# The tail of a two-layer graph network: the sums of the next tile ordered ahead of W's product, additions on VectorE, and a second set of row buffers

## Chip, cores and metric

One Trainium2 chip, one core, one program. The metric is the device time of one execution in microseconds: the median of three runs is 2738.88 us (2735.98 to 2744.72).

## The reference, cut to what matters

x has 32 batches of 512 nodes with 512 features; adj is one random 512 x 512 matrix with about four neighbours per node. There are two layers, each behind a layernorm and a relu, each added to x:

```python
# layer 0: masked attention, 8 heads of 64
h = maximum(layernorm(x), 0)
x = x + softmax(q k^T / 8 + (1 - adj) * -1e9) v  @ Wo
# layer 1: graph attention with a multiplied mask
h = maximum(layernorm(x), 0)
hw = h @ W;  s1 = hw @ a1;  s2 = hw @ a2
e = leaky_relu(s1[:, None] + s2[None, :], 0.2) * adj
x = x + elu(softmax(e) @ hw + beta * hw)
```

In layer 1 the mask multiplies e, so nodes that are not neighbours weigh exp(0) = 1. The kernel writes the weighted sum as the sum of all states of the batch plus, for each neighbour, (exp(e) - 1) times its state, and puts the product with W after the sum.

## The kernel before, in words

**Tiles.** A batch has four tiles of 128 nodes. For each tile the kernel gathers, from tables in device memory, the rows of its nodes' neighbours (GpSimd's indirect DMAs, L946, four a tile, into two "kv" buffers), and in layer 0 also the queries (L968, four a tile, into two "qe" buffers). A row of the table holds K, V and, from column HO on, the layer-1 part: one score and the 512 values of the state h, padded to HW_ = 520 columns (ROW = 1552).

**Periods.** `stage_b` runs through periods b = 0 to 33. Period b works on layer 0 of batch b and layer 1 of batch b - 2 (LAG = 2), tile by tile; tile n is 4b + t. The last two periods, tiles 128 to 135, have layer 1 alone, of batches 30 and 31, and gather the state rows only, from the table th.

**Layer 1 of a tile** (`edge_weights`, `layer1`):
- VectorE adds s1 to the gathered score (L1127, once per kv buffer), leaky relu (L1131); ScalarE exp (L1133); VectorE completes z (L1134), copies it into the rows where layer 0 needs it (L1138) and spreads it to the weights wv (L1140).
- TensorE multiplies wv with the gathered states, four matmuls with 32 columns of weights each (L987, "sums"), and in the last two periods wv with ones (L42 128x1, "count").
- VectorE makes the denominator (L1162 to L1164, "den") and adds the tile's own state (L1170, "own"). ScalarE had put its relu into the same buffer (L756).
- TensorE turns the result (L737, four transposes). ScalarE adds the column sums of the batch, cs, in four instructions of 128x128 (L1181, `add_all`) and so brings it to SBUF as gT.
- TensorE multiplies gT with W (L42, 128x512, eight matmuls). ScalarE scales in two passes (L1190, L1191, `halves`), VectorE does elu and adds x (L1195, L1196), GpSimd issues the store (L767, `keep`).

**Layer 0 of a tile**: product with the queries (L1000), reduction (L1003), exp (L1009), V weighed on ScalarE (L1014), sums "px" (L987), division (L1042, L1038), transposes, oT copied by ScalarE (L1051), product with wo (L42), addition (L1053), layernorm (L744 to L751, with its pow on GpSimd, L749), relu (L756), scores (L1061) and the store into the table. When all four tiles of a batch are through, `self_sums` adds up its states on TensorE (L1081) and cs is reduced (L1087); `spread_s1` sends the scores s1 through memory (SP, L1103 and L1108) to the form in which z needs them (L1112, L1113).

**What sets the order.** Every operation is given to a planner (`Plan`, L65 to L215) with its engine, an estimated time, a key (its due time), and the buffers it reads and writes. A tile has S = 20 of key: tile n begins at kb = base(n) = 100 + 20n. `order` runs a greedy list schedule over the estimated times and takes on each engine the ready operation with the lowest key; what comes out is the fixed order of each engine. Buffers come from rings: five "kv", two "qe", four "w", six PSUM banks "D", one "gT", one "oT", two "wv". On PSUM's ring any free one is taken, on the other rings allocations follow the keys. TensorE's list has a preference for staying with matmuls of the same form (32 or 128 rows).

Before the change the keys of layer 1 are: gathers kb - 17, z kb + 12 (0.6 S), sums, count, den, own kb + 20 (S), transposes and addition kb + 29.7 (+ 0.485 S), product kb + 37.6 (+ 0.88 S), halves and elu kb + 41 (+ 1.05 S), store kb + 44.

Of the kernel before, what the change touches and what calls it, by code (L numbers as in the profile page):

```python
# [12 lines left out]
ALU = mybir.AluOpType  # L13
# [6 lines left out]
P = 128  # L20
# [7 lines left out]
G = 32  # L28
# [1 line left out]
MAXDEG = 16  # L30
VW = 65
KO, VO, HO = 0, 512, 512 + 8 * VW
HW_ = 520
ROW = HO + HW_
QW = 516
LAG = 2
# [182 lines left out]
def kernel(  # L219
# [486 lines left out]


    S = 20.0
    AHEAD = 6

    def base(n):
# [222 lines left out]
    def stage_b(b):  # L934

        s = st[b] if b < B else None
        old = st[b - LAG] if b >= LAG else None
        if old is not None:
            old["dn"] = buf("dn", f"dn{b}")
        if s is not None:  # L940
            s["x1"], s["hx"] = [None] * T, [None] * T
            s["mv1"], s["s1"] = buf("mv1", f"mv1_{b}"), buf("s1", f"s1_{b}")
            s["rd"] = buf("rd", f"rd{b}")

        def gather(dst, tab, t, g):
            nc.gpsimd.indirect_dma_start(  # L946
                dst, None, tab.ap, bass.IndirectOffsetOnAxis(ap=idx[:, t, g : g + 1], axis=0),
                bounds_check=N + DUMMY - 1, oob_is_err=False,
            )

        for t in range(T):
            kb = base(T * b + t)
            slots = [buf("kv", f"kv{b}_{t}_{i}") for i in range(2)]
            held = [{n: buf(None, n) for n in ("K", "V", "H")} for _ in range(2)]
            of = {KO: "KVH", VO: "VH", HO: "H"}
            for g in range(NG):
                for tab, c0, c1 in st[b]["tab"]:
                    op("POOL", 1.3, kb - 0.85 * S + 0.1 * g, lambda sl=slots[g // 2], g=g, t=t, tab=tab, c0=c0, c1=c1: gather(
                        sl.ap[:, g % 2, c0:c1], tab, t, g),
                       r=[tab, C_["idx"]],  # L960
                       w=[(slots[g // 2], (g % 2, c0)), *((held[g // 2][n], (g % 2, "row")) for n in of[c0])],
                       dma=P * (c1 - c0) * 4)
            if s is not None:
                qs = [buf("qe", f"qe{b}_{t}_{i}") for i in range(2)]
                for q in qs:
                    q.q, q.s1 = buf(None, "q"), buf(None, "s1")
                for g in range(NG):
                    op("POOL", 1.3, kb - 0.84 * S + 0.1 * g, lambda q=qs[g // 2], g=g, t=t: nc.gpsimd.indirect_dma_start(  # L968
                        q.ap[:, g % 2, :], None, s["qtab"].ap,
                        bass.IndirectOffsetOnAxis(ap=qidx[:, t, g : g + 1], axis=0),  # L970
                        bounds_check=N, oob_is_err=False),
                       r=[s["qtab"], C_["qidx"]], w=[(x, g % 2) for x in (qs[g // 2], qs[g // 2].q, qs[g // 2].s1)],
                       dma=P * QW * 4)
            wvb = edge_weights(b - LAG, t, kb, slots, held, qs if s is not None else None) if old is not None else None
            pv = layer0(b, t, kb, slots, held, qs, old is not None) if s is not None else None
            if old is not None:
                layer1(b - LAG, t, kb, slots, held, wvb, pv)
                if t == T - 1:
                    op("DVE", 0.16, kb + 1.6 * S, lambda: nc.vector.tensor_tensor(
                        dmax, dmax, old["dn"].ap[:, 0:2, :], op=ALU.max), r=[old["dn"]], w=[C_["dmax"]])  # L980
        if s is not None:
            self_sums(b, base(T * b + 6))
# [136 lines left out]
    def edge_weights(b, t, kb, slots, held, qs):  # L1119

        s = st[b]
        k1 = kb + 0.6 * S
        z, wvb = buf("z", f"z{b}_{t}"), buf("wv", f"wv{b}_{t}")
        for i in range(2):
            def add(i=i):
                s1 = s["s1e"].ap[:, t, 2 * i : 2 * i + 2] if qs is None else qs[i].ap[:, :, D]
                nc.vector.tensor_tensor(z.ap[:, 2 * i : 2 * i + 2], s1, slots[i].ap[:, :, HO], op=ALU.add)  # L1127

            op("DVE", 0.2, k1, add, r=[*([s["s1e"]] if qs is None else [(qs[i], "use"), qs[i].s1]),
                                       *use([slots[i]], [held[i]], "H")], w=[z])  # L1130
        op("DVE", 0.2, k1, lambda: nc.vector.scalar_tensor_tensor(  # L1131
            z.ap, z.ap, ALPHA, z.ap, op0=ALU.mult, op1=ALU.max), w=[z])
        op("ACT", 0.25, k1, lambda: nc.scalar.activation(z.ap, z.ap, AF.Exp), w=[z])  # L1133
        op("DVE", 0.2, k1, lambda: nc.vector.scalar_tensor_tensor(  # L1134
            z.ap, z.ap, -1.0, nzE[:, t, :], op0=ALU.add, op1=ALU.mult), r=[C_["nzE"]], w=[z])
        if b + LAG < B:
            for i in range(2):
                op("DVE", 0.1, k1, lambda i=i: nc.vector.tensor_copy(  # L1138
                    slots[i].ap[:, :, HO], z.ap[:, 2 * i : 2 * i + 2]), r=[z, (slots[i], "use")], w=[(held[i]["H"], "z")])
        op("DVE", 0.35, k1, lambda: nc.vector.tensor_tensor(  # L1140
            wvb.ap.rearrange("p (g r) -> p g r", r=G), oh[:, ts(t, NG), :],
            z.ap.unsqueeze(2).to_broadcast([P, NG, G]), op=ALU.mult), r=[z, C_["OH"]], w=[wvb])
        return wvb

    def layer1(b, t, kb, slots, held, wvb, pv):
        s = st[b]
        px, g = buf("D", f"pg{b}_{t}"), buf("w", f"g{b}_{t}")
        o = op("PE", 1.02, kb + S, lambda: edge_sums(
            lambda i: px.ap[ts(i, G), :], lambda i: wvb.ap[:, ts(i, G)], slots, HO + 1, D),
               r=[*((x, "use") for x in slots), *((h["H"], "rows") for h in held), wvb], w=[px], form=4)  # L1150
        plan.reserve(o, g)
        k = kb + S
        x1, dn = s["x1"][t], s["dn"]
        op("ACT", 0.8, k, lambda: relu(g.ap, x1.ap, s["mv1"].ap, t), r=[x1, (s["mv1"], t)], w=[g])

        if pv is None:
            pd = buf("D", f"pn{b}_{t}")
            op("PE", 0.2, kb + S, lambda: product(nc, pd.ap[:, 0:1], wvb.ap, one32[:, 0:1]), r=[wvb], w=[pd])

        def den():  # L1160
            src, by = (pd.ap[:, 0:1], float(G)) if pv is None else (pv.ap[:, 1, 4 * VW : 4 * VW + 1], 1.0)
            nc.vector.tensor_scalar(dn.ap[:, 0, t : t + 1], src, by, float(N), op0=ALU.mult, op1=ALU.add)  # L1162
            nc.vector.reciprocal(dn.ap[:, 1, t : t + 1], dn.ap[:, 0, t : t + 1])
            nc.vector.tensor_scalar(  # L1164
                dn.ap[:, 2, t : t + 1], dn.ap[:, 0, t : t + 1], beta_b, 1.0, op0=ALU.mult, op1=ALU.mult)

        op("DVE", 0.5, k, den, r=[pd if pv is None else pv], w=[(dn, t)])

        def own():
            nc.vector.scalar_tensor_tensor(  # L1170
                g.ap, g.ap, dn.ap[:, 2, t : t + 1], px.ap, op0=ALU.mult, op1=ALU.add
            )

        op("DVE", 0.75, k, own, r=[px, (dn, t)], w=[g])
        pt, gT, py, y = buf("D", "pt"), buf("gT", f"gT{b}_{t}"), buf("D", "py"), buf("w", f"y{b}_{t}")
        oo = op("PE", 0.45, k + 0.485 * S, lambda: turned(pt.ap, g.ap), r=[g], w=[pt])
        plan.reserve(oo, gT)

        def add_all():
            for c in range(C):  # L1180
                nc.scalar.activation(  # L1181
                    gT.ap[:, c, :], pt.ap[:, ts(c, P)], AF.Identity, bias=s["cs"].ap[:, c : c + 1]
                )

        op("ACT", 1.5, k + 0.485 * S, add_all, r=[pt, s["cs"]], w=[gT])
        oo = op("PE", 3.43, k + 0.88 * S, lambda: dense(py.ap, gT.ap, w1), r=[gT, C_["w1"]], w=[py])
        plan.reserve(oo, y)

        def halves():
            nc.scalar.activation(y.ap, py.ap, AF.Exp, scale=dn.ap[:, 1, t : t + 1])  # L1190
            nc.scalar.activation(py.ap, py.ap, AF.Relu, scale=dn.ap[:, 1, t : t + 1])  # L1191


        def elu():
            nc.vector.scalar_tensor_tensor(y.ap, y.ap, 1.0, x1.ap, op0=ALU.min, op1=ALU.add)  # L1195
            nc.vector.tensor_tensor(y.ap, y.ap, py.ap, op=ALU.add)  # L1196

        op("ACT", 1.36, k + 1.05 * S, halves, r=[(dn, t)], w=[py, y])
        op("DVE", 1.45, k + 1.05 * S, elu, r=[py, x1], w=[y])
        op("POOL", 1.3, k + 1.2 * S, lambda: keep(y.ap, b, t), r=[y, C_["perm"]], dma=P * D * 4)  # L1200

    def judge():
        ok, okm = buf("q", "ok"), buf("w", "okm")
# [245 lines left out]
```

## Time and profile before

| | us |
|---|---|
| median of three runs | 2738.88 |
| the profiled execution, its own time | 2723.47 |
| its span from first to last instruction | 2721.6 |
| TensorE busy | 2648.3 (97%) |
| VectorE busy | 2049.9 (75%) |
| ScalarE busy | 1934.4 (71%) |
| GpSimd busy | 1831.2 (67%) |
| last product with W ends | 2711.3 |

The granted TensorE clock is 0.99 of full speed over the span. The DMA engines moved 790 MB at a mean of 290 GB/s; most of it is gathered rows. Two parts of the span look different from the rest. From 1000 to 2480 us TensorE has no idle time. In the last 160 us it has idle time in every stretch of 40 us. The tile 127, the last of layer 0, has its product with W done at 2646.15; the eight products with W of the last two periods follow up to 2711.3. A line of the page or the trace gives the engine, the line of kernel.py, the operation, the operands as out<-in with their shape, and in brackets the idle time ahead of it on its engine with what ended it.

### The profile page before, as it was taken

How to read it: one execution, taken by the hardware profiler on the slowest of the kernel's cores; microseconds unless marked ns; L12 is line 12 of the kernel's file. 1: busy time of each engine (PE TensorE's matmuls, PEld its weight loads, DVE VectorE, ACT ScalarE, POOL GpSimd, SP SyncE). 2: the span in 40 equal slices, each digit the busy share in tenths (PEclk: the TensorE clock that was granted, in tenths of full speed). 3: DMA queues.
4: the chain of work that ended last, by engine and by line, in shares of the span. 5: the costliest groups of instructions: out<-in, count | busy, mean ns of one | idle time of the engine just before them, and what ended most of it. 6: DMA issues, size and time to landing. Idle time of an engine off the chain costs nothing.

```text
span 2721.6 us, 39762 instructions
## 1 busy us (share of the span) xinstructions
PE 2648.3 (97%) x10220; PEld 1213.2 (45%) x10220; DVE 2049.9 (75%) x5200; ACT 1934.4 (71%) x6215; POOL 1831.2 (67%) x1710
## 2 busy tenths in 40 slices
PE   8999999999999999999999999999999999999886
PEld 4444444444444444444444444444444444444332
DVE  7768777777777777777777777777777777777663
ACT  1557777687877777777777777777777777777763
POOL 2776766666766766766766776676676676675763
PEclk9999999999999999999999999999999999999988
DMA  5988998888988988988988988988888888888863
GB/s 180 252 290 320 307 307 291 297 294 305 311 296 289 321 292 296 314 297 288 316 298 292 326 291 290 321 289 303 312 296 292 305 309 303 297 310 286 303 211 117
DMA packets 237457, 790.08 MB, mean 290 GB/s; under 512 B 34667, under 2 KB 34675, under 8 KB 237222
## 3 DMA queue, kind: packets, MB, share of 16 engines
q0 software_dynamic: 156736, 644.99, 70.3%
q1 hardware_dynamic: 80486, 142.48, 14.0%
q8 instruction: 83, 1.36, 0.2%
q14 instruction: 152, 1.25, 0.1%
HBM read 617.88 MB, written 169.46 MB: 289 GB/s over the span
## 4 chain that ended last, share of the span: by engine, by line
PE 88%; DMA 3%; issue 3%; DVE 2%; ACT 2%; POOL 2%; POOLq 0%; SPq 0%; DVEq 0%; ACTq 0%
PE pd L42 46%; PE pd L858 26%; PE pd L737 6%; PE pd L987 4%; PE px L987 4%; DMA qe<-qtab,qidx 1%; ACT kv L1014 1%; PE pd L918 1%; DMA kv<-tkv,idx 1%; PE pd L1081 1%; POOL kv L946 1%; POOL qe L968 0%; POOL x L762 0%; DMA x<-in_x_dram,perm 0%; DVE s L1003 0%
## 5 line engine op out<-in xcount | busy, mean ns | idle before, releaser
L1014 ACT ACTIVATE kv<-kv 128x64 f32<-128x64 f32 x4096 | 1011.8, 335 | 5.2
L968 POOL DMA_INDIRECT qe<-qtab,qidx x512 | 556.0, 1086 | 223.0 <-issue 114.0
L946 POOL DMA_INDIRECT kv<-tab,idx x480 | 508.2, 1059 | 164.6 <-issue 113.6
L42 PE MATMUL pd<-wo,oT 128*128 128x512 f32 x1032 | 468.6, 597 | 2.5 <-ACT oT L1051 2.4
L42 PE MATMUL pd<-w,gT 128*128 128x512 f32 x1024 | 466.1, 598 | 3.6 <-ACT gT L1181 3.6
L42 PE MATMUL pd<-wq,hT 128*128 128x512 f32 x1024 | 465.0, 597 | 2.2 <-ACT hT L782 2.2
L762 POOL DMA_INDIRECT x<-in_x_dram,perm x252 | 359.5, 1426 | 85.1 <-issue 50.3
L1000 DVE TENSOR_TENSOR qe<-qe,kv 128x1024 f32<-128x1024 f32 x256 | 312.1, 1220 | 44.4 <-DMA qe<-qtab,qidx 35.6
L1003 DVE TENSOR_REDUCE s<-qe 128x16 f32<-128x1024 f32 x256 | 310.5, 1214 | 0.1
L42 PEld LDWEIGHTS pd<-w,gT 128*128 128x128 f32 x1024 | 195.7, 192 | 249.5 <-issue 234.0
L42 PEld LDWEIGHTS pd<-wo,oT 128*128 128x128 f32 x1032 | 196.3, 192 | 245.0 <-issue 222.0
L42 PEld LDWEIGHTS pd<-wq,hT 128*128 128x128 f32 x1024 | 195.4, 192 | 245.6 <-issue 241.7
L749 POOL TENSOR_TENSOR mv<-mv,mhalf 128x1 f32<-128x1 f32 x256 | 171.4, 670 | 177.5 <-DVE mv L746 156.7
L767 POOL DMA_INDIRECT out_dram<-w,perm x128 | 157.3, 1229 | 149.8 <-DVE w L1196 105.7
L858 PE MATMUL pd<-wk,hT 128*128 128x512 f32 x496 | 239.7, 607 | 3.7 <-ACT hT L782 3.4
L858 PE MATMUL pd<-wt,S 128*128 128x512 f32 x496 | 238.5, 603 | 4.5 <-DVE k L866 4.1
L858 PE MATMUL pd<-wv,S 128*128 128x512 f32 x496 | 233.6, 593 | 3.1 <-DVE v L866 1.8
L1190 ACT ACTIVATE w<-pd,dn 128x512 f32<-128x512 f32 x128 | 87.6, 684 | 185.8 <-PE pd L42 185.5
L1061 DVE CUSTOM_DVE_ANT_0 w<-hx,wa_r 128x512 f32<-128x512 f32 x256 | 175.1, 684 | 11.3 <-ACT hx L756 10.5
L1053 DVE TENSOR_TENSOR x<-pd,x 128x512 f32<-128x512 f32 x128 | 87.9, 687 | 121.8 <-PE pd L42 110.1
L744 DVE BATCH_NORM_STATS2 st<-x 128x6 f32<-128x512 f32 x256 | 176.3, 689 | 3.8 <-DMA x<-in_x_dram 1.0
L737 PE MATMUL pd<-ident,w 128*128 128x128 f32 x1152 | 154.3, 276 | 21.7 <-DVE w L1038 11.2
(204 smaller groups left out, 3504.7 us busy)
## 6 DMA issues: line engine op xcount, KB each, us to landing
qtab<-q SPq DMA_DIRECT2D x124, 258.0 KB
tab<-hx SPq DMA_DIRECT2D x120, 260.0 KB
tab<-v SPq DMA_DIRECT2D x120, 260.0 KB
tab<-k SPq DMA_DIRECT2D x120, 256.0 KB
qe<-qtab,qidx POOLq DMA_INDIRECT x512, 7.8
kv<-tab,idx POOLq DMA_INDIRECT x480, 8.0
x<-in_x_dram,perm POOLq DMA_INDIRECT x252, 8.0
th<-hx SPq DMA_DIRECT2D x8, 260.0 KB
```

The source lines that it names most:

```text
L42: nc.tensor.matmul(out, lhsT, rhs, start=start, stop=stop)
L737: nc.tensor.transpose(p[:, ts(c, P)], src[:, ts(c, P)], ident)
L744: nc.vector.bn_stats(s6.ap, src.ap)
L762: nc.gpsimd.indirect_dma_start(dst, None, rows, bass.IndirectOffsetOnAxis(ap=perm[:, t : t + 1], axis=0), **lim)
L858: nc.tensor.matmul(p.ap, lhs()[:, c, :], rhs[:, c, :], start=first and c == 0, stop=c == K2 - 1, skip_group_check=True)
L946: nc.gpsimd.indirect_dma_start(dst, None, tab.ap, bass.IndirectOffsetOnAxis(ap=idx[:, t, g : g + 1], axis=0), bounds_check=N + DUMMY - 1, ...
L968: op("POOL", 1.3, kb - 0.84 * S + 0.1 * g, lambda q=qs[g // 2], g=g, t=t: nc.gpsimd.indirect_dma_start(q.ap[:, g % 2, :], None, s["qtab"]. ...
L987: nc.tensor.matmul(out(g), lhs(g), slots[g // 2].ap[:, g % 2, c0 : c0 + n], start=True, stop=True)
L1000: nc.vector.tensor_tensor(qe.ap[:, :, 0:D], qe.ap[:, :, 0:D], sl.ap[:, :, KO : KO + D], op=ALU.mult)
L1003: nc.vector.tensor_reduce(sb.ap, qe.ap[:, :, 0:D].rearrange("p n (h f) -> p n h f", f=HD), axis=AX.X, op=ALU.add)
L1014: nc.scalar.activation(p[:, h, 0:HD], p[:, h, 0:HD], AF.Copy, scale=p[:, h, HD : HD + 1])
L1061: nc.vector.tensor_tensor_reduce(scr.ap, hx.ap[:, 1 : D + 1], row, 1.0, 0.0, op0=ALU.mult, op1=ALU.add, accum_out=dst)
```

## The change

It has four parts, all but the first for the last two periods only:

1. HW_ 520 becomes 516, so ROW 1548: the row of the table is 6192 bytes instead of 6208.
2. New keys (GL = 0.5, ZL = 0.2): z kb + 4, sums, count, den and own kb + 10, transposes and addition kb + 12, product kb + 34, halves and elu kb + 35, store kb + 38. The sums of tile n + 1 (kb + 30) so come due before the product of tile n.
3. The addition of cs is one VectorE instruction of 128x512 (`add_at_once`, cs broadcast) and no longer four of ScalarE.
4. Odd tiles take the two "qe" buffers for their rows and the "oT" ring for gT; the rows then begin at column 0 of the buffer (`slots.ho`).

```diff
-HW_ = 520
+HW_ = 516
...
+            alone = s is None and t % 2 == 1
+            slots = [buf("qe" if alone else "kv", f"kv{b}_{t}_{i}") for i in range(2)]
+            for sl in slots:
+                sl.ho = 0 if alone else HO
...
-                        sl.ap[:, g % 2, c0:c1], tab, t, g),
+                        sl.ap[:, g % 2, c0 - HO + sl.ho : c1 - HO + sl.ho], tab, t, g),
...
-        k1 = kb + 0.6 * S
+        k1 = kb + (0.6 if b + LAG < B else ZL) * S
...
+        last = b + LAG >= B
+        k = kb + (GL if last else 1.0) * S
+        kt, kw, ke = (0.6 - GL, 1.7 - GL, 1.75 - GL) if last else (0.485, 0.88, 1.05)
...
-        pt, gT, py, y = buf("D", "pt"), buf("gT", f"gT{b}_{t}"), buf("D", "py"), buf("w", f"y{b}_{t}")
+        pt, gT, py, y = buf("D", "pt"), buf("oT" if last and t % 2 else "gT", f"gT{b}_{t}"), buf("D", "py"), buf("w", f"y{b}_{t}")
...
+        def add_at_once():
+            nc.vector.tensor_tensor(
+                gT.ap, pt.ap.rearrange("p (c q) -> p c q", c=C), s["cs"].ap.unsqueeze(2).to_broadcast([P, C, P]), op=ALU.add)
+        if last:
+            op("DVE", 0.72, k + kt * S, add_at_once, r=[pt, s["cs"]], w=[gT])
+        else:
+            op("ACT", 1.5, k + kt * S, add_all, r=[pt, s["cs"]], w=[gT])
+        oo = op("PE", 3.43, k + kw * S, lambda: dense(py.ap, gT.ap, w1), r=[gT, C_["w1"]], w=[py])
```

The planner turns this into a new order on TensorE. With s for sums, c for count, t for transposes, W for the product with W (o for layer 0's), from the product of tile 126 on:

```
before: W126 s127 px127 c128 t127 o127 W127 s128 c.. t128 W128 s129 c.. t129 W129 s130 ... t135 W135
after:  W126 s127 px127 c128 s128 t127 o127 W127 c129 t128 c130 s129 W128 t129 s130 W129 t130 c131 s131
        W130 t131 c132 s132 W131 t132 c133 s133 W132 t133 c134 s134 W133 t134 c135 s135 W134 t135 W135
```

In the period before (tiles 124 to 127), VectorE's order changes too: the weights wv of tiles 126 and 127 stand behind the elu of tiles 125 and 126, where they stood ahead of it. On GpSimd, the first ten gathers from th stand ahead of the pow of tile 126, where it was six. In the rest of the program the change of the row's length alters what the planner estimates for the DMAs, and neighbouring operations change places here and there; the number of changes between matmuls of 32 and of 128 rows goes from 281 to 291.

More of the change, by code (lines that the diff above doesn't have):

```diff
@@ L708 @@
     S = 20.0
+    GL, ZL = 0.5, 0.2
     AHEAD = 6
@@ L952, in stage_b @@
             kb = base(T * b + t)
-            slots = [buf("kv", f"kv{b}_{t}_{i}") for i in range(2)]
+            alone = s is None and t % 2 == 1
+            slots = [buf("qe" if alone else "kv", f"kv{b}_{t}_{i}") for i in range(2)]
+            for sl in slots:
+                sl.ho = 0 if alone else HO
             held = [{n: buf(None, n) for n in ("K", "V", "H")} for _ in range(2)]
@@ L1126, in add @@
                 s1 = s["s1e"].ap[:, t, 2 * i : 2 * i + 2] if qs is None else qs[i].ap[:, :, D]
-                nc.vector.tensor_tensor(z.ap[:, 2 * i : 2 * i + 2], s1, slots[i].ap[:, :, HO], op=ALU.add)
+                nc.vector.tensor_tensor(z.ap[:, 2 * i : 2 * i + 2], s1, slots[i].ap[:, :, slots[i].ho], op=ALU.add)
             op("DVE", 0.2, k1, add, r=[*([s["s1e"]] if qs is None else [(qs[i], "use"), qs[i].s1]),
@@ L1146, in layer1 @@
         s = st[b]
+        last = b + LAG >= B
+        k = kb + (GL if last else 1.0) * S
+        kt, kw, ke = (0.6 - GL, 1.7 - GL, 1.75 - GL) if last else (0.485, 0.88, 1.05)
         px, g = buf("D", f"pg{b}_{t}"), buf("w", f"g{b}_{t}")
-        o = op("PE", 1.02, kb + S, lambda: edge_sums(
-            lambda i: px.ap[ts(i, G), :], lambda i: wvb.ap[:, ts(i, G)], slots, HO + 1, D),
+        o = op("PE", 1.02, k, lambda: edge_sums(
+            lambda i: px.ap[ts(i, G), :], lambda i: wvb.ap[:, ts(i, G)], slots, slots[0].ho + 1, D),
                r=[*((x, "use") for x in slots), *((h["H"], "rows") for h in held), wvb], w=[px], form=4)
         plan.reserve(o, g)
-        k = kb + S
         x1, dn = s["x1"][t], s["dn"]
@@ L1157, in layer1 @@
             pd = buf("D", f"pn{b}_{t}")
-            op("PE", 0.2, kb + S, lambda: product(nc, pd.ap[:, 0:1], wvb.ap, one32[:, 0:1]), r=[wvb], w=[pd])
+            op("PE", 0.2, k, lambda: product(nc, pd.ap[:, 0:1], wvb.ap, one32[:, 0:1]), r=[wvb], w=[pd])
         def den():
@@ L1174, in layer1 @@
         op("DVE", 0.75, k, own, r=[px, (dn, t)], w=[g])
-        pt, gT, py, y = buf("D", "pt"), buf("gT", f"gT{b}_{t}"), buf("D", "py"), buf("w", f"y{b}_{t}")
-        oo = op("PE", 0.45, k + 0.485 * S, lambda: turned(pt.ap, g.ap), r=[g], w=[pt])
+        pt, gT, py, y = buf("D", "pt"), buf("oT" if last and t % 2 else "gT", f"gT{b}_{t}"), buf("D", "py"), buf("w", f"y{b}_{t}")
+        oo = op("PE", 0.45, k + kt * S, lambda: turned(pt.ap, g.ap), r=[g], w=[pt])
         plan.reserve(oo, gT)
@@ L1183, in add_all @@
                 )
-        op("ACT", 1.5, k + 0.485 * S, add_all, r=[pt, s["cs"]], w=[gT])
-        oo = op("PE", 3.43, k + 0.88 * S, lambda: dense(py.ap, gT.ap, w1), r=[gT, C_["w1"]], w=[py])
+        def add_at_once():
[6 more added lines that the diff above has]
+        oo = op("PE", 3.43, k + kw * S, lambda: dense(py.ap, gT.ap, w1), r=[gT, C_["w1"]], w=[py])
         plan.reserve(oo, y)
@@ L1196, in elu @@
             nc.vector.tensor_tensor(y.ap, y.ap, py.ap, op=ALU.add)
-        op("ACT", 1.36, k + 1.05 * S, halves, r=[(dn, t)], w=[py, y])
-        op("DVE", 1.45, k + 1.05 * S, elu, r=[py, x1], w=[y])
-        op("POOL", 1.3, k + 1.2 * S, lambda: keep(y.ap, b, t), r=[y, C_["perm"]], dma=P * D * 4)
+        op("ACT", 1.36, k + ke * S, halves, r=[(dn, t)], w=[py, y])
+        op("DVE", 1.45, k + ke * S, elu, r=[py, x1], w=[y])
+        op("POOL", 1.3, k + (ke + 0.15) * S, lambda: keep(y.ap, b, t), r=[y, C_["perm"]], dma=P * D * 4)
     def judge():
```

## The prediction, made before the changed kernel was run

> **What bounds the kernel now.** I read the page's slices first, then the windows by stage, then TensorE's timeline of the end, last the list of waits and VectorE's timeline there.
>
> ```profile
> PE   8999999999999999999999999999999999999886
> ...
> DVE  7768777777777777777777777777777777777663
> ...
> DMA  5988998888988988988988988988888888888863
> ```
>
> Slices are 68 us. TensorE is at nine tenths everywhere but in the first and the last three. The windows give this in us (columns: stretch, its length, then busy time and instructions of TensorE, weight loads, VectorE, ScalarE, GpSimd; granted clock, DMA share, GB/s).
>
> ```profile
> 2000.00:2480.00 480.00, 480.00 (x1879) 220.66 (x1878) 371.87 (x939) 360.14 (x1159) 329.69 (x307) 1.00 0.87 301
> ...
> 2560.00:2600.00 40.00, 28.57 (x110) 12.76 (x108) 26.78 (x66) 28.52 (x98) 30.90 (x28) 0.91 0.96 328
> 2600.00:2640.00 40.00, 32.20 (x145) 14.76 (x146) 27.92 (x85) 31.14 (x103) 25.32 (x21) 0.84 0.61 190
> 2640.00:2680.00 40.00, 33.28 (x115) 13.61 (x113) 18.56 (x63) 15.12 (x37) 24.29 (x25) 0.90 0.63 177
> 2680.00:2722.00 42.00, 24.36 (x89) 9.67 (x88) 13.29 (x43) 13.29 (x31) 11.24 (x11) 0.89 0.23 71
> ```
>
> From 1000 to 2480 us TensorE has no gap: there only its own work counts. From 2560 on it has gaps and its clock falls. The change aims at the last eight tiles (128 to 135), which lie between the end of W's product of tile 127 (2646.15) and that of tile 135 (2711.31), 65.2 us. Two tiles of it on TensorE (start, length, line, operands, count; in brackets the idle time before and its releaser):
>
> ```profile
> 2669.74 1.06 PE L987 MATMUL pd<-kv,wv 128*32 128x512 f32 x8
> 2670.73 0.38 PE L42 MATMUL pd<-one,wv 128*128 128x1 f32 x2
> 2673.72 0.66 PE L737 MATMUL pd<-ident,w 128*128 128x128 f32 x4 [2.61 <-DVE w L1170]
> 2674.90 5.40 PE L42 MATMUL pd<-w,gT 128*128 128x512 f32 x8 [0.52 <-ACT gT L1181]
> 2680.22 1.07 PE L987 MATMUL pd<-kv,wv 128*32 128x512 f32 x8
> 2681.22 0.38 PE L42 MATMUL pd<-one,wv 128*128 128x1 f32 x2
> 2682.32 0.66 PE L737 MATMUL pd<-ident,w 128*128 128x128 f32 x4 [0.72 <-DVE w L1170]
> 2683.49 3.70 PE L42 MATMUL pd<-w,gT 128*128 128x512 f32 x8 [0.52 <-ACT gT L1181]
> ```
>
> Every tile is one serial chain: sums, count, wait for VectorE's own (L1170), transposes, wait for ScalarE's addition (L1181), product. The idle times before the rows of the stretch are .71, .52, 1.25, .58, .52, 2.61, .52, .72, .52, 2.61, .52, .72, .52, 1.03, .51: 13.9 us. The products take 3.60 to 3.70 after short gaps and 5.30 or 5.40 (three of them) after long ones: 5.2 us more. So 65.2 is 13.9 of gaps, 5.2 of slow clock and 46.1 of work. The waits that feed these gaps:
>
> ```profile
> DVE z L1127 <- DMA kv<-th,idx: 20.8, 9, 3.8
> ...
> POOL kv L946 <- PE pd L42: 13.3, 6, 4.2
> ...
> PE pd L737 <- DVE w L1170: 9.0, 7, 2.6
> ```
>
> The addends of z wait for gathered rows, and the gathers for buffers that TensorE frees. Since VectorE works in order, the wait holds what is behind it (2669.74's own was done only at 2673.6, behind den, elu and a late elu of the tile before):
>
> ```profile
> 2671.15 0.16 DVE L1162 TENSOR_SCALAR dn<-pd 128x1 f32<-128x1 f32 x1 [3.66 <-PE pd L42]
> ...
> 2671.54 0.68 DVE L1195 SCALAR_TENSOR_TENSOR w<-w,x 128x512 f32<-128x512 f32 x1
> 2672.32 0.69 DVE L1196 TENSOR_TENSOR w<-w,pd 128x512 f32<-128x512 f32 x1
> 2672.93 0.74 DVE L1170 SCALAR_TENSOR_TENSOR w<-w,dn,pd 128x512 f32<-128x512 f32 x1
> ```
>
> [...]
>
> **The change part by part.** I sum against the profiled execution, 2723.47 us (span 2721.6); the median of the runs is 2738.88, 15.4 above it, and I carry differences over unchanged.
>
> Without any gap and at full clock, the stretch holds, from start to start: 8 transposes at .50, 8 products at 3.53, 7 sums at .89, 7 counts at .28, and .98, .27, .50 of batch 31's column sums and turned rows (2653.93 to 2655.64): 4.0 + 28.2 + 6.2 + 2.0 + 1.8 = 42.1. Of sums and counts, tile 128's go ahead of the stretch, into the 1.16 us gap at 2636.06. So the ceiling is 42.1 - 65.2 = **-23.1 us**.
>
> The emitted order of the changed kernel gives back (order only, durations from the trace):
> - Product n now stands behind sums n + 1, so own and the addition of tile n are covered by 1.17 us (sums, count) and 3.53 (product). The addition is one VectorE instruction (.60 to .75; I take L1196's .69) for four of ScalarE (1.14, TensorE starting .52 after). Covered it costs nothing; the last tile's has no cover, **+0.9** with the hand-over.
> - In VectorE's order, weights wv of tile 131 stand behind the addition of 130: count and sums 131 wait, **+1.1**. The addition of 132 stands behind z of 134, whose gather is queued on GpSimd behind the output of tile 130: **+0.7**.
> - wv of 132 stands behind elu of 130, wv of 135 behind elu of 133. Each needs, after product n ends, ScalarE's first half (.69), two elu passes (.69 + .69), z's completion (.16), wv (.29), and some .9 in hand-overs: 3.4 after product n, of which the transposes cover .5: **+2.9** and **+3.0**.
> - Products after these two gaps run at the slow clock, 5.3 for 3.6: **+3.4**.
> - Ten more changes between 32-row and 128-row matmuls, over the whole program, at .1 (the first four of L858 after such a change take 1.98 for 1.88): **+1.0**.
> - In period 31, where layer 0 is still on the path, wv of 126 and 127 have also slipped behind elu of 125 and 126. Before, wv came first (2616.84 ahead of 2617.12). First half, two elu, copy and wv come to 2.8 to 3.1 after the product; sums 126 waited .92 already, sums 127 nothing: +1.8 and +2.9, and half of the slow-clock loss that sums and px showed at 2602.13 (3.4 for 2.0), .7: **+5.4**.
> - Odd tiles' rows in the q rows' two buffers relieve the 13.3 us of buffer waits: gathers start earlier. GpSimd issues the same 32 gathers at a pitch of 1.31 us, so these alone could be done near 2671 instead of 2690; I count this as what allows the -23.1, not twice. ZL (z at 0.2) is likewise in the order above. SP's order in the tail doesn't change; GpSimd's puts ten gathers of 128 to 130 ahead of the pow of 126, where six were: within the ±2 for period 31.
> - Row 520 to 516: .26% fewer bytes in the wide rows[...]. I take 0, since TensorE covers 0.87. The steady order is reshuffled; its gaps sum to 6.7 us from 500 on: -4 to +4, taken 0.
>
> Sum of what is given back: .9 + 1.1 + .7 + 2.9 + 3.0 + 3.4 + 1.0 + 5.4 = 18.4. Net **-4.7**: profile 2718.8, median 2734.2.
>
> **Rivals.** *The clock stays full and period 31 absorbs its slip.* [...] (before, a gap of 1.25 + .58 was followed by 5.40, against it; one of .71 + .52 by 3.70, for it). Then +3.4 and .7 fall away, and if the earlier gathers let elu and wv close up, 3.5 of the slip too: -12.3, 2726.6; -19 if half of the other waits go. *Nothing in the end:* the stretch is set by batch 31's s1 row (L1103, L1108, L1112), which the change doesn't move: 2739. For it: z 132 needs it; against: L1112 came at 2664.86, 2 us ahead of its reader. *Slower:* gathered rows land later. The addends of z are moved to 0.2, so VectorE stands sooner at the head of its queue for rows that now share the engines with layer 0's; before, rows of th landed 3.4 at least, 3.8 in the middle and 7.2 at most after issue. At 7 instead of 3.6 the z of four tiles would hold own, den or layer 0's scale by 3.5 each: +14, net +9.3, 2748.2. It decides from about 5 us; DMA at 0.96 around 2580 speaks for it, 0.61 after 2600 against.
>
> **How the numbers follow.** About 0.3% (8.2 us) is what a measurement of this kernel can tell from no change. Forecast (2734.2; own range 2730 to 2739): .43; faster rival .38; nothing .06; slower .13. Its lower half and steady-order gains put .40 under 2730.7; .47 is within 0.3%; .13 slower. The range runs from 2720 (most of the faster case, -19) to 2747 (most of the slower).
>
> **What would show it.** Right: TensorE's row for sums n + 1 ahead of each product; no gap ahead of products but the last; gaps of about 3 us at counts 132 and 135 released by L1140's counterpart; slower products after them; sums 126 and 127 some 2 and 3 us behind the product. The clean stretch between 1000 and 2480 stays without gaps. Wrong: the stretch from product 127 to 135 far from 65.2 - 23.1 + 12 = 54, z waits over 5 us, or gaps in the steady part.

## The result, and the profile after

Over 17 runs each the changed kernel took 2750.21 us (2742.48 to 2756.72) and the kernel before 2739.56 us: a ratio of 1.0035 (1.0025 to 1.0045), where 2734.2 was forecast. Its profiled execution took 2746.48 us, span 2744.6.

One thing about the numbers has to be known first. The runs of this case were made in seven series, each with its own runs of the kernel before. Before's median in them was 2739.6, 2734.8, 2734.1 and 2733.6 in four ("upper level"), 2725.5, 2725.1 and 2724.8 in three ("lower level"). All ratios are within a series. The trace of before that the prediction was read from took 2723.47. That lies inside the range of before's runs in the lower series (2721.42 to 2731.96) and under every one in the upper series (2729.11 at least), so it is counted to the lower level; the changed kernel's first trace, 2746.48, is one of the runs of the first, upper series. The record names the chip of the six series of experiments: chips 7 (twice) and 4 in the upper level, 9, 3 and 11 in the lower. So the level may go with the chip, and the two series on chip 7 agree within 1 us; that the chip sets it is not shown, since only one chip came twice.

The slices of the changed kernel, to set beside those of before:

```profile
PE   8999999999999999999999999999999999999976
...
DVE  7767777777777777777777777777777777777674
...
DMA  5988898988889888988888888888888988988873
```

They show nothing: TensorE is at 9 tenths as it was. The windows of the changed kernel do (same columns as in the prediction; "x" and a number are instructions):

```profile
500.00:1000.00 500.00, 496.05 (x1923) 227.48 (x1924) 376.27 (x957) 362.68 (x1163) 334.19 (x316) 1.00 0.87 296
1000.00:1500.00 500.00, 490.52 (x1898) 223.78 (x1897) 376.21 (x958) 368.77 (x1197) 338.50 (x317) 1.00 0.86 295
1500.00:2000.00 500.00, 497.72 (x1918) 226.74 (x1916) 382.66 (x967) 371.61 (x1201) 342.54 (x319) 1.00 0.87 300
2000.00:2480.00 480.00, 480.00 (x1883) 221.01 (x1883) 372.14 (x934) 359.12 (x1154) 330.77 (x310) 1.00 0.87 301
...
2660.00:2700.00 40.00, 32.70 (x141) 15.27 (x141) 21.67 (x74) 12.81 (x27) 22.59 (x21) 0.91 0.51 148
2700.00:2745.00 45.00, 28.32 (x98) 12.08 (x98) 19.38 (x61) 10.32 (x19) 13.36 (x13) 0.83 0.25 82
```

and those of the kernel before, for the same stretches:

```profile
500.00:1000.00 500.00, 493.62 (x1912) 225.86 (x1911) 381.25 (x971) 378.51 (x1235) 342.29 (x322) 1.00 0.87 302
1000.00:1500.00 500.00, 500.00 (x1975) 230.30 (x1974) 386.53 (x973) 373.65 (x1196) 346.26 (x321) 1.00 0.86 298
1500.00:2000.00 500.00, 500.00 (x1957) 230.03 (x1956) 389.02 (x982) 370.87 (x1192) 347.78 (x323) 1.00 0.87 303
```

Between 1000 and 2000 TensorE now idles 11.8 us (9.48 and 2.28), where it idled none. So much of the loss lies where the change was not aimed. The px sums of tile 122 (layer 0's) start at 2581.4 against 2554.2, the last product ends at 2734.3 against 2711.3. The end itself became shorter, 60.0 us from product 127 to product 135 for 65.2. Its middle on TensorE:

```profile
2682.91 3.60 PE L42 MATMUL pd<-w,oT 128*128 128x512 f32 x8
2686.34 0.60 PE L738 MATMUL pd<-ident,w 128*128 128x128 f32 x4
2690.73 0.38 PE L42 MATMUL pd<-one,wv 128*128 128x1 f32 x2 [3.79 <-issue]
2691.04 1.06 PE L992 MATMUL pd<-qe,wv 128*32 128x512 f32 x8
2692.04 5.40 PE L42 MATMUL pd<-w,gT 128*128 128x512 f32 x8
2697.27 0.60 PE L738 MATMUL pd<-ident,w 128*128 128x128 f32 x4
2702.56 0.59 PE L42 MATMUL pd<-one,wv 128*128 128x1 f32 x2 [4.68 <-DVE wv L1145]
```

Sums stand ahead of the product (2691.04 ahead of 2692.04), and no product waits but the last (0.78 us), as the change has it. The rest of the waiting has gathered at three counts, 131 (3.79; "issue" means that the profile shows no releaser), 132 (4.68) and 135 (2.84). The products after the first two run at 5.40 and 5.87, the one after the third at 3.70; the granted clock over them is 0.68, 0.63 and 1.00.

### The profile page after: what moved, and what is told of

The parts are those of the page before. It is cut to its first block, busy times and chain, and to the rows that moved or that the text cites. A ratio compares the mean times of both kernels' runs of the same rounds, so it can differ in the third digit from the quotient of the medians.

```text
span 2744.6 us, 39734 instructions
## 1 busy us (share of the span) xinstructions
PE 2656.2 (97%) x10220; PEld 1213.7 (44%) x10220; DVE 2052.4 (75%) x5208; ACT 1926.7 (70%) x6183; POOL 1819.1 (66%) x1710
## 4 chain that ended last, share of the span: by engine, by line
PE 89%; DVE 3%; issue 3%; DMA 2%; POOL 1%; ACT 1%; another core or an unknown queue 0%; POOLq 0%; SPq 0%; DVEq 0%; ACTq 0%
PE pd L42 46%; PE pd L859 27%; PE pd L738 6%; PE pd L992 4%; PE px L992 4%; DMA qe<-qtab,qidx 1%; PE pd L919 1%; PE pd L1086 1%; POOL kv L947 0%; ACT kv L1019 0%; DVE s L1008 0%; POOL x L763 0%; DVE qe L1005 0%; POOL qe L973 0%
## 5 line engine op out<-in xcount | busy, mean ns | idle before, releaser
L973 POOL DMA_INDIRECT qe<-qtab,qidx x512 | 547.5, 1069 | 244.2 <-issue 119.3
L947 POOL DMA_INDIRECT kv<-tab,idx x480 | 522.8, 1089 | 200.8 <-issue 121.4
L42 PE MATMUL pd<-w,gT 128*128 128x512 f32 x992 | 448.0, 594 | 0.0
L763 POOL DMA_INDIRECT x<-in_x_dram,perm x252 | 353.0, 1401 | 96.2 <-issue 54.4
L42 PEld LDWEIGHTS pd<-w,gT 128*128 128x128 f32 x992 | 188.7, 191 | 239.8 <-issue 225.9
L738 PEld LDWEIGHTS pd<-ident,w 128*128 128x128 f32 x1152 | 133.6, 142 | 102.2 <-issue 57.3
```

What stands on the lines that cost most here:

```text
L42: nc.tensor.matmul(out, lhsT, rhs, start=start, stop=stop)
L738: nc.tensor.transpose(p[:, ts(c, P)], src[:, ts(c, P)], ident)
L763: nc.gpsimd.indirect_dma_start(dst, None, rows, bass.IndirectOffsetOnAxis(ap=perm[:, t : t + 1], axis=0), **lim)
L947: nc.gpsimd.indirect_dma_start(dst, None, tab.ap, bass.IndirectOffsetOnAxis(ap=idx[:, t, g : g + 1], axis=0), bounds_check=N + DUMMY - 1, ...
```

## The experiments

Ratios are to before in the same series, with the 95% interval.

**1. Which part of the change costs: the row, its order or its bytes, or the tail (upper level).** The planner is told each transfer's bytes. So memory and order can be set apart:

```diff
# row516: before with
-HW_ = 520
+HW_ = 516
# order516_row520: before with the planner told 516
-dma=P * (c1 - c0) * 4)
+dma=P * (c1 - c0 + (-4 if c1 == ROW else 0)) * 4)
-dma=P * HW_ * 4)
+dma=P * 516 * 4)
# order520_row516: HW_ = 516, the planner told 520 (same two places, not shown)
# tail520: after with HW_ = 520 and the q rows' buffers 520 wide (not shown)
```

> The kernel before with the row of 516 alone; nothing of the last two periods changed. The two traces differ by 27.2 us ahead of tile 122's sums (14.9 of gaps on TensorE, 12.3 of longer work), and by 10.7 in the medians. Theory A (the planner, fed other DMA sizes, writes a worse steady order): about 2755, 0.5 to 0.6% slower than before, with new gaps between 1000 and 1800 us. Theory B (rows of 6192 bytes are slower to move): the same time, since this run doesn't separate the two. Theory C (the loss is in the tail and period 31, and the profile of before was a lucky one): 2740, no difference.

> The kernel before with rows of 520 in memory, but the planner told 516: the order on each engine is that of the run with the row of 516 alone, instruction for instruction. Theory A (order): as slow as that run, about 2755. Theory B (bytes): as the kernel before, 2740.

> The opposite: rows of 516 in memory, the planner told 520, so the order of the kernel before. Theory A: 2740, no difference. Theory B: about 2755.

> The whole change of the last two periods (keys, VectorE's addition, second buffers) with rows of 520; the q rows' buffers are made 520 wide so that the rows fit. The order up to tile 127's sums is that of before on TensorE. Theory A or B: the tail's gain alone is left, the stretch from product 127 to product 135 goes from 65.2 to about 60 as in the changed kernel's trace or less, and tiles 126 and 127 don't slip: 2725 to 2733. Theory C: slower than before, about 2750.

Measured: row516 1.0065 (1.0048 to 1.0082), order516_row520 1.0070 (1.0057 to 1.0083), order520_row516 0.9999 (0.9991 to 1.0007), tail520 0.9973 (0.9966 to 0.9981). Theory A holds, B and C fall. The traces show that memory and order were indeed set apart: TensorE, VectorE, ScalarE and GpSimd go through the same sequence of instructions in row516 and in order516_row520, and again the same one in before and in order520_row516. Before and row516 part from one another at 310 us. The bytes cost nothing that these runs can tell: rows of 6208 and of 6192 bytes take 282 and 281 ns of a DMA engine each (mean of the packets between 500 and 1800 us, order516_row520 and row516). The loss comes with the order that the planner writes when it is told four columns fewer, and the change of the last two periods by itself is a gain.

**2. The changed kernel with the old steady order, and its parts (lower level).**

```diff
# after_est520: after with the planner told 520 for rows of 516 (not shown)
# elu_late: also elu of tiles 130 and 133 behind the weights of 132 and 135 (not shown)
# add_act: also the addition on ScalarE
-        if last:
+        if False:
# no_qe: also no second buffers
-            alone = s is None and t % 2 == 1
+            alone = False
```

> The changed kernel as it is, rows of 516 in memory, with one difference: the planner is told the transfer sizes of rows of 520, so the steady order is that of the kernel before. If the order is the whole loss, this is as fast as the run of the last two periods alone with rows of 520: ratio to before 0.9973, about 2727.5 where before is 2735. If rows of 516 cost something together with the new tail: 2735 or more.

> As the run after_est520, with the elu of tiles 130 and 133 put behind the weights of tiles 132 and 135 in VectorE's order. If the waits at counts 132 and 135 come from these elu passes, as the prediction has it (+2.9 and +3.0, and a slow product after each): the 2.84 gap at count 135 falls to under 0.6 and its product runs at full clock, the gap at count 132 shortens by 1.4 or more; 4 to 8 us faster than after_est520. If the weights wait for gathered rows or for s1 anyway: no difference.

> As the run after_est520, but the addition of the column sums stays on ScalarE in four pieces in the last two periods too; keys and buffers as changed. The prediction costs the move at nothing where sums and count cover it (1.17 us of cover against 1.14): within 2 us of after_est520. If the move to VectorE puts work in the way of the weights (131, 132): this is 1 to 4 us faster; if ScalarE's halves stand in its way: 2 to 6 slower.

> As the run after_est520, but all tiles keep the five kv buffers (the oT ring for odd tiles' gT stays). The prediction counts the second buffers as what allows the gain of the new order: then rows come late again, z waits for them, and the stretch of the last eight tiles goes back to 64 us or more, 3 to 8 us slower than after_est520. If the buffers did not bound it: within 1.5 us.

Measured: after_est520 0.9967 (0.9954 to 0.9979), elu_late 0.9964 (0.9951 to 0.9977), add_act 0.9964 (0.9952 to 0.9976), no_qe 0.9953 (0.9939 to 0.9967). With either VectorE's addition or the second buffers taken away, the gain stays. So neither adds anything that these runs can tell while the other is there, and what all four share is the new keys, with the oT ring for odd tiles' gT. No run has the keys alone. That the second buffers are "what allows the -23.1" is refuted: without them VectorE's z still waits 15.2 us for gathered rows in the last 270 us (20.8 in before, 10.6 in after_est520), and the stretch from product 127 to product 135 is 54.0 us all the same (54.5 in after_est520). So these waits did not set the length of the stretch. The end of after_est520 on TensorE is the tail that the prediction drew:

```profile
2663.70 0.38 PE L42 MATMUL pd<-one,wv 128*128 128x1 f32 x2 [1.02 <-DVE wv L1145]
...
2671.80 0.38 PE L42 MATMUL pd<-one,wv 128*128 128x1 f32 x2 [2.65 <-DVE wv L1145]
2672.11 1.94 PE L992 MATMUL pd<-kv,wv 128*32 128x512 f32 x8
2673.97 4.47 PE L42 MATMUL pd<-w,oT 128*128 128x512 f32 x8
...
2692.08 0.38 PE L42 MATMUL pd<-one,wv 128*128 128x1 f32 x2 [2.84 <-DVE wv L1145]
2692.39 1.77 PE L992 MATMUL pd<-qe,wv 128*32 128x512 f32 x8
2694.09 4.65 PE L42 MATMUL pd<-w,gT 128*128 128x512 f32 x8
2698.57 0.60 PE L738 MATMUL pd<-ident,w 128*128 128x128 f32 x4
2699.96 3.70 PE L42 MATMUL pd<-w,oT 128*128 128x512 f32 x8 [0.78 <-DVE oT L1194]
```

The wait at count 135 is the elu in front of the weights in VectorE's queue (after_est520, VectorE):

```profile
2690.15 0.68 DVE L1210 SCALAR_TENSOR_TENSOR w<-w,x 128x512 f32<-128x512 f32 x1
2690.94 0.69 DVE L1211 TENSOR_TENSOR w<-w,pd 128x512 f32<-128x512 f32 x1
2691.54 0.15 DVE L1139 SCALAR_TENSOR_TENSOR z<-z,nzE 128x4 f32<-128x4 f32 x1
2691.73 0.29 DVE L1145 TENSOR_TENSOR wv<-OH,z 128x128 f32<-128x128 f32 x1
```

In elu_late the weights come first, and the wait at that count shortens; what is left is the addition and z (TensorE):

```profile
2691.36 0.38 PE L42 MATMUL pd<-one,wv 128*128 128x1 f32 x2 [1.80 <-DVE wv L1147]
2691.68 1.07 PE L992 MATMUL pd<-qe,wv 128*32 128x512 f32 x8
2692.67 3.70 PE L42 MATMUL pd<-w,gT 128*128 128x512 f32 x8
```

The two waits fell from 2.65 and 2.84 to 1.62 and 1.80, and both products after them ran at 3.70. But a wait of 2.21 came up at count 133, where there was none: there z waited 1.85 us for gathered rows. The expected 4 to 8 us did not come: 1.0 us in the stretch, nothing in the ratio. So the elu was what came last at these counts, but other work, rows among it, came close behind. no_qe has one wait of 6.02 at count 132 instead of several.

**3. Other numbers told to the planner (upper level).** As order516_row520, with 512 and 524.

> The kernel before with rows of 520 in memory and the planner told 512; nothing else. If a smaller transfer estimate is worse as such (rows thought to come earlier than they do): slower than with 516 told, ratio to before over 1.007. If each reshuffle of the order is a draw of its own: anywhere between 0.997 and 1.01, with gaps in other places between 500 and 1800 us.

> The same with 524 told. If a larger estimate is the safe side: ratio 1.000 or under. If each reshuffle is a draw of its own, and the order with 520 a kept good one: above 1.002.

Measured: 1.0043 (1.0028 to 1.0058) and 1.0017 (1.0009 to 1.0026), the second a little under the 1.002 expected of a draw. Neither direction is the safe one; each of the three other numbers gives another order, and each is slower than with 520.

**4. A last combination, and the changed kernel again (lower level).** no_qe with elu of tile 130 late; after unaltered.

> As the run no_qe, with elu of tile 130 put behind the weights of tile 132. Before, count 132 waited 6.02 us, of which the two elu passes ahead of the weights are 1.4 and the rest is gathered rows (VectorE's z waited 2.17 and .77 for them). If elu counts: the gap falls to about 4.5 and its product runs at full clock, 1.4 to 2.5 us faster than no_qe, ratio to before 0.9945. If rows alone set it: no difference, 0.9953.

> The changed kernel once more, unaltered, for a second profile. In the first, counts 131 and 132 waited 3.79 and 4.68 us, where the prediction had 1.1 and 2.9 and the run after_est520, with the same order of these tiles, showed 1.02 and 2.65. If the extra is of that execution alone: 1.0 and 2.7 here, and a stretch of 54 to 55 us. If it belongs to the kernel: 3.8 and 4.7 again, 60 us. In both cases tile 122's sums come 18 to 27 us later than in the kernel before.

Measured: no_qe_elu 0.9972 (0.9962 to 0.9983). Its wait at count 132 is still 6.03, so rows set it (z waited 2.15 and 2.11 for them); the planner, given one constraint more, put elu of 133 ahead of the weights of 135 again, a wait of 2.57. after_again gave 0.9977 (0.9967 to 0.9987): here the same kernel is faster than before. Its stretch was 53.9 us, with waits of 1.32, 2.84, 2.84 and 0.78; px of tile 122 started at 2563.5.

**5. Does the order cost the same everywhere?** Four kernels again, unaltered, in one series (it fell in the upper level), and two in another (lower).

> The row of 516 alone once more (steady order reshuffled, tail as before). If before takes about 2725 here: theory P (the order's cost depends on where it runs) has 1.001 to 1.003 instead of 1.0065; theory Q (the order costs the same, the tail gains more) has 1.006. If before takes 2734 or more: 1.0065 again under both.

> The changed kernel, unaltered. Where before takes 2725: 0.9977 again. Where before takes 2735 to 2740: 1.0035 again. Under theory P its difference to row516_b is the tail's gain, 0.003 to 0.004, in both.

> The changed kernel with the steady order of before. 0.9967 again, wherever it runs, if the tail's gain does not depend on the place; after_c lies above it by what the order costs in this place: 0.001 where before takes 2725, 0.006 where it takes 2735 or more.

> The changed kernel with the steady order of before and without the second row buffers. The first time 0.9953 against 0.9967 with them, intervals overlapping. If the buffers are worth nothing: within 0.001 of after_est520_b again.

> The row of 516 alone, a third time. Measured so far: 1.0065 and 1.0075, both where before took 2734. If before takes about 2725 here and the order's cost depends on the place: 1.001 to 1.004. If before takes 2725 and it is 1.006 or more: the order costs the same everywhere and the 0.9977 of the changed kernel stays unexplained. If before takes 2733 or more again: 1.007, and the question stays open.

> The changed kernel with the steady order of before, a third time: 0.9956 to 0.9967 wherever it runs.

Measured, upper: row516_b 1.0075 (1.0062 to 1.0089), after_c 1.0022 (1.0015 to 1.0030), after_est520_b 0.9956 (0.9942 to 0.9970), no_qe_b 0.9959 (0.9946 to 0.9973). Lower: row516_d 1.0044 (1.0030 to 1.0058), after_est520_d 0.9971 (0.9961 to 0.9981). So theory P in part: the order's cost depends on the level (18 to 21 us in the upper, 12 in the lower, a little more than was expected), while the tail with the old order gains 7 to 12 us in the upper and 8 to 9 in the lower. The intervals of the single runs of row516 overlap between the levels; the traces below part them more clearly. Under theory P after_c was to lie 0.003 to 0.004 under row516_b; it lies 0.0053 under.

What the order does is seen from the traces (us; start of tile 122's px, the gaps that TensorE's timeline lists, and from tile 127's px to the end of the last product):

| trace | order, level | tile 122 | gaps 100-1000 | gaps 1000-1800 | px 127 to end |
|---|---|---|---|---|---|
| before | 520, lower | 2554.2 | 17.7 | 0 | 77.8 |
| after_est520 | 520, lower | 2558.4 | 18.1 | 0 | 66.3 |
| order520_row516 | 520, upper | 2561.0 | 22.2 | 0 | 77.4 |
| tail520 | 520, upper | 2561.2 | 18.1 | 0 | 72.9 |
| row516_d | 516, lower | 2559.6 | 15.5 | 4.1 | 81.4 |
| after_again | 516, lower | 2563.5 | 13.5 | 4.2 | 66.2 |
| row516 | 516, upper | 2576.3 | 17.4 | 10.5 | 83.0 |
| after | 516, upper | 2581.4 | 21.5 | 11.3 | 71.9 |
| after_c | 516, upper | 2578.2 | 16.4 | 11.3 | 70.2 |

With the old order TensorE has no gap from 1000 to 1800 at either level. With the new one it has, and they grow with the level. The gaps are not the whole loss. From px of tile 56 to px of tile 88 every trace holds the same 2528 matmuls. They take 647.2 to 647.3 us with the old order at the lower level and 647.8 at the upper; with the new order they take 650.5 and 650.9 at the lower level and 655.9 to 658.3 at the upper. Of these +3.4 and +9.1 us (means) only 1.5 to 1.8 and 4.7 to 5.7 are listed gaps.

The largest gap, in row516 (upper level, tile 52):

```profile
1149.06 1.06 PE L987 MATMUL px<-kv,OH 128*32 128x260 f32 x16
1150.05 1.98 PE L858 MATMUL pd<-wt,S 128*128 128x512 f32 x4
1155.30 0.66 PE L737 MATMUL pd<-ident,w 128*128 128x128 f32 x4 [3.27 <-DVE dn L1162]
```

and the same instructions in row516_d (lower level):

```profile
1144.65 1.06 PE L987 MATMUL px<-kv,OH 128*32 128x260 f32 x16
1145.64 1.98 PE L858 MATMUL pd<-wt,S 128*128 128x512 f32 x4
1147.81 0.66 PE L737 MATMUL pd<-ident,w 128*128 128x128 f32 x4 [0.19 <-DVE w L1038]
```

Only one group of four matmuls (1.98) stands between px and the transposes that need the division of its result; even in the good case 0.19 is missing. The old order has 12 to 20 matmuls there in each of the tiles 32 to 87, the new one only 4 or 8 in twelve of these 56 tiles. This number is no price, though: with 512 told it is two such tiles (ratio 1.0043), with 524 ten (1.0017). VectorE, in row516, was ready and waited for px (the releaser "remote" is one that the profile could not name):

```profile
1150.96 0.15 DVE L746 TENSOR_SCALAR mv<-mv 128x1 f32<-128x1 f32 x1
1154.10 0.21 DVE L1042 RECIPROCAL rd<-px 128x8 f32<-128x8 f32 x1 [2.99 <-remote]
```

and in row516_d:

```profile
1146.63 0.20 DVE L1042 RECIPROCAL rd<-px 128x8 f32<-128x8 f32 x1
```

In row516 px began at 1149.06 and is written as ending by 1150.12, yet its reader started at 1154.10, 5.04 us after px began; in row516_d the reader started 1.98 us after. The wait at count 131 looks to be of the same kind: about 1 us at the lower level (1.02, 0.98, 1.32), 3.73 to 3.79 in after, after_c and after_est520_b (2.12 in tail520). In after, the addition ahead of these weights on VectorE waited for its transposes:

```profile
2689.79 0.69 DVE L1194 TENSOR_TENSOR gT<-pd,cs 128x512 f32<-128x512 f32 x1 [3.08 <-remote]
```

It started 3.45 us after the transposes (2686.34); in after_est520 it started 0.64 us after them.

## Why the prediction was wrong, point by point

- **The failed step** is "The steady order is reshuffled; its gaps sum to 6.7 us from 500 on: -4 to +4, taken 0". It bounded what a new order can add by the gaps that the old one had. The measured term is +17.8 us (row516, 0.0065 x 2734.8), +20.5 (row516_b) and +12.0 (row516_d, lower level). Of it some 13 (upper: five traces start px of tile 122 at 2578.2 in the mean, four with the old order at 2564.8) or 5 (lower: two traces at 2561.5, seven at 2556.9) lie ahead of tile 122. The part from tile 56 to tile 88 is the firm one, +9.1 and +3.4; the rest lies ahead of tile 56, where the traces of one order and one level already differ by 3 to 9 us. Another 3.6 to 5.6 lie in the old tail itself (81.4 to 83.0 for 77.4 and 77.8), which the full change replaces. Why the matmuls of the new order follow each other less closely where no gap is listed stays open.
- **Bytes taken at 0**: right, by order520_row516 (0.9999).
- **The tail**: right in where TensorE waits and, at the lower level, nearly in size. The forecast stretch was 65.2 - 23.1 + 12.0 = 54.1; measured 54.5 (after_est520), 53.9 (after_again) and 56.7 (after_est520_d). Its terms in after_est520: count 131 +1.1 (1.02), count 132 +2.9 (2.65), count 135 +3.0 (2.84), the last addition +0.9 (0.78). The +0.7 for the addition of 132 did not come, and count 130 waited 0.76 that was not in the sum: that these two cancel is luck. Two slow products were put at +3.4, by the products of 5.30 and 5.40 in before's trace (granted clock 0.69 and 0.68 over them, 1.00 over those of 3.70 at 2649.42 and 2683.49); sums and products after the waits show 1.94 for 1.06 and 4.47 for 3.70, and 1.77 and 4.65: together 3.3. In after_est520_d, after the same waits, they show 4.6. At the upper level the stretch was 58.5 to 61.2, since count 131 waited more (3.73 to 3.79, in tail520 2.12) and in after and after_c also count 132 (4.68 and 3.10); without the second buffers it was 55.2 there (no_qe_b), which the runs don't show as a gain (0.9959 and 0.9956).
- **Period 31, +5.4**: mis-sized. The waits of sums 126 and 127 for their weights came (2.57 and 3.37 in after), but they took the place of waits that before had there (0.92, 2.16 and two slow products with wo). From px 122 to the end of product 127 it is 93.0 in after for 91.9 in before, +1.1; it is 0 from before to after_again, both lower, and +2.3 from order520_row516 to after, both upper. The slip belongs to the steady order too: row516, with the tail's keys unchanged, has the two waits as well (2.57 and 2.83).
- **Second buffers, VectorE's addition**: taken at nothing in cost, which holds; the buffers were taken as needed, which fails. With it falls the reading that z's waits for rows set the gaps of the stretch: no_qe has 15.2 us of such waits, one wait of 6.02 on TensorE comes from them, and the stretch is as short.
- **Rivals.** The slower rival (late rows, +9.3) named the wrong mechanism: z's waits for rows of th are 3.6 us in all in after's last 270 us and 12.2 in after_again's, where they were 20.8. Its "7.2 at most" for rows of th is a misreading: that gather reads the wide table, and the five from th whose landing before's trace shows took 3.4 to 5.3. The faster rival had -12.3 and the forecast -4.7; the last two periods alone gained 7.4 (tail520) to 12.0 (after_est520_b). Of the rival's grounds, the clock did not stay full (0.68 and 0.63 granted over after's products of 5.40 and 5.87; in after_est520 products of 4.47 and 4.65 for 3.70), while period 31 did absorb most of its slip. Behind the same wait of 2.84 at count 135 the product took 3.70 in after, 4.65 in after_est520 and 5.40 in after_c: these runs show no length of wait from which a product is slow. No rival was "the planner writes a worse steady order".
- **The carried difference.** The 15.4 us between profile and median were taken as a constant. By the ranges given above they were the two levels, and the new order loses more at the level at which the runs were made than at that of the trace.

In one sum (us, upper level): order ahead of tile 122 about +13, from there to px of tile 127 +2 to +3 (80.0 and 81.0 for 78.1 in order520_row516), tail -7 to -5.5 (70.2 and 71.9 for 77.4): about +8 (after_c) and +10 (after), measured +6.0 and +9.6. Lower level: +5, 0 (79.4 for 79.3) and -11.6 (66.2 for 77.8): -6.6, measured -6.3 (after_again, 0.0023 x 2725.1).

Open: why TensorE's results reach their readers some 3 us later at some places of the upper level (5.04 us after px began in row516 for 1.98 in row516_d, 3.45 after the transposes in after for 0.64 in after_est520), and what sets the levels. From 500 to 1800 us the mean durations on VectorE, ScalarE and GpSimd and the time per packet of a table row (280 to 283 ns) agree within 1.2% between the levels.

## What to carry to other kernels

An order that a planner writes is one of the change's parts: a number that only feeds its estimates, here four columns of 1552, can cost more (12 to 21 us) than the edit it comes with gains (7 to 12). Hold the order fixed with the old estimate and change one thing at a time; and do not bound what a new order can cost by the gaps of the old one. The slack that it leaves between a result and its reader on the bounding engine is the place to look, though these runs give no price for it. A profile that is faster than every run shown beside it may come from another condition, as it did here, and differences read from it must be checked in the runs' own.

## What was not expected of the hardware

- The same kernel's medians lay 8 to 15 us apart between series (2724.8 to 2725.5, and 2733.6 to 2739.6), and the sign of the change went with it: 0.9977 and 1.0035.
- A row of 6192 bytes was moved as fast as one of 6208 (281 ns a packet in row516, 282 in order516_row520, 500 to 1800 us).
- From tile 88 to tile 112 each eight tiles took 161.8 us at the lower level and 161.9 to 162.2 at the upper, whatever the order: the order's loss lies ahead of this part and behind it.
